# Attention and mixture of experts on one core: all batches projected from raw x, a rebuilt opening, and row normalisation moved to GpSimd

## The chip, the core and the metric

The kernel runs on one core of a Trainium2 chip. The core has five engines with queues of their own: TensorE (PE in the profile, its weight loads PEld), VectorE (DVE), ScalarE (ACT), GpSimd (POOL) and SyncE (SP, which issues most of the DMAs). Each works through its queue in order and waits for the others by semaphores. The metric is the device time of one execution in microseconds (us), the median of several runs.

## What is computed

The input x has 16 batches of 512 tokens of 128 features, float32. Cut to what matters:

```python
xn = layernorm(x)                       # no gain, no bias
q, k, v = xn @ Wq, xn @ Wk, xn @ Wv     # 16 heads of 8
q, k = q / |q|, k / |k|                 # per head
o = causal_softmax(8 * q @ k.T) @ v     # per head
attn = o @ Wo
probs = softmax(xn @ Wr.T)              # 8 experts
top_v, top_i = top_k(probs, 2); top_v = top_v / sum(top_v)
ffn = sum over the two experts e:  top_v[e] * (gelu(xn @ W1[e].T + b1[e]) @ W2[e].T + b2[e])
out = x + attn + ffn
```

## The kernel before, in words

**Layer norm by two roads.** The mean is taken out of the weights: `centre` (L325) subtracts the columns' means from `wall` (Wq, Wk, Wv side by side) and from the router's `wr_sb`. Batches 0 to 3 (`b < RAW`) are normalised row by row first (`normalise`, L302), turned by TensorE (`turn_x`, L315) and projected; their copies out of PSUM are plain. Batches 4 to 15 arrive a second time as 32x32 squares (`load_squares`, L120), are turned in place by VectorE (`turn_raw`, L321), and projected raw; `rstd` is a scale of the copy out (L675). Every batch's normalised rows are still wanted in `rows`, since these are the rows that go to the experts. `stats` (L237) takes the statistics of one batch on VectorE (four instructions), and `scales` (L264) makes `rstd` and `shift` of a range of batches: `variance`, then the root by ScalarE's Sqrt and a reciprocal, or (`root=False`) by a logarithm and an exponential and one Newton step.

**Preparing a batch** (`prep`, L653): `proj` of four pieces of 128 tokens (TensorE, copied out by ScalarE), `squares` of queries and keys (GpSimd), `values` into `vaug` (GpSimd), `sums` of squares, `root`, `root_step` and `scale` (VectorE and ScalarE), then `turn_q` and `turn_k` (transposes on TensorE, copied by VectorE), and `alone`, which makes from the turned keys one copy for each of four groups of heads.

**The loop over stages.** A batch's attention is PER = 10 stages; stage t belongs to batch t // 10. In each, `scores` (L757) runs the `sim` matmuls and two exponentials on ScalarE (L787), `mask` (L803) zeroes the upper triangles of the diagonal blocks of the stage before, on GpSimd or, for some stages, on VectorE, and `weigh` (L821) multiplies two stages later by the values into the one bank `av`, which VectorE then turns into `mid` (L833). A mask goes to VectorE only when the list `router` is empty. The order on every engine is the order in which this program is written: `at_stage(t, step)` puts a step into `plan`, and `due(t)` runs the steps of stage t after its `weigh`. `prep(b)` places its steps from eighteen stages before the batch to one after its start. The list `side` gives one step to each stage from 0 on: turns of x and, for groups of four batches, `logits` (matmuls with the router's weights) and `turn_logits`. Projections, transposes and logits share one PSUM bank, `misc`; scores and some early steps rotate over three double banks (`SIM`).

**The router.** `route` (ten steps) picks two experts for each token, `place` (eight steps, then `later`) counts them and gives each row its slot. A list of (stage, steps) spreads these over stages 20 to 38, nearly all of it VectorE's. From stage 40 on, `stage` takes one or two of 128 `sends` (indirect DMAs by GpSimd that write `rows` to the slots in DRAM). GpSimd's work runs in the order of issue (`on_pool`, L592). Before stage 138 the last sends are flushed, and SP starts to fetch the experts' blocks (L898 to L919), which wait for all sends. The experts run before stage 140 (`hidden`, L950, and `mix`, L964), and the last two batches' attention and the combination end the kernel.

**The opening.** Ahead of stage 0 stands an order written out by hand for batch 0 (`zero`): statistics, normalisation by ScalarE and VectorE, transposes, projection, norms, turned queries and keys, and in between statistics of batches 1 to 7 and normalisation of batches 1 to 4. `keep_busy` runs matmuls whose results nobody reads. `InstLoadActFuncSet` (L1168) loads the function table for the exponentials.

Of the kernel before, what the change touches and what calls it, by code (L numbers as in the profile page):

```python
# [24 lines left out]
def attention_moe_kernel(  # L25
# [276 lines left out]
    def normalise(b, engines):  # L302

        for c, engine in enumerate(engines):
            i = b * NC + c
            to, what = rows[b][:, c, :D], x_sb[b][:, c]
            by, less = rstd[:, i : i + 1], shift[:, i : i + 1]
            if engine is nc.scalar:
                nc.scalar.activation(to, what, AF.Identity, bias=less, scale=by)
            elif engine is nc.vector:  # L310
                nc.vector.tensor_scalar(to, what, by, less, ALU.mult, ALU.add)
            else:
                on_pool(nc.gpsimd.tensor_scalar, to, what, by, less, ALU.mult, ALU.add)

    def turn_x(b, bank, copy):  # L315

        for c in range(NC):
            nc.tensor.transpose(bank[:, ts(c, P)], rows[b][:, c, :D], ident)
        copy(xnT[b], bank)  # L319
# [5 lines left out]
    def centre():  # L325

        means = SIM("means")
        for w, first in ((wall, 0), (wr_sb, NQKV)):
# [3 lines left out]
        return lambda: [  # L332
            nc.vector.scalar_tensor_tensor(
# [8 lines left out]
    def logits(b0):  # L342
# [7 lines left out]
        nc.vector.tensor_copy(ltT, lt)  # L350

    def turn_logits(b0):
# [6 lines left out]
        if b0 < RAW:  # L359
            nc.vector.tensor_copy(to, what)  # L360
        else:
            by = rstd[:, b0 * NC : (b0 + GB) * NC].rearrange("p (g c) -> p c g", g=GB)
            nc.vector.tensor_mul(
                to, what, by.unsqueeze(3).to_broadcast([P, NC, GB, E])
            )
# [292 lines left out]
    def prep(b):  # L658
# [5 lines left out]
        def proj(c, bank=misc):  # L664
# [6 lines left out]
            if b < RAW:  # L671
                nc.scalar.copy(s["qkv"][:, c], pp[:, :NQKV])  # L672
            else:
                i = b * NC + c
                nc.scalar.activation(  # L675
                    s["qkv"][:, c], pp[:, :NQKV], AF.Identity, scale=rstd[:, i : i + 1]
                )
# [18 lines left out]
        def sums():  # L696
            s["ss"] = sm.tile([P, n], F32, tag="ss", name=f"ss{b}", bufs=1)
            nc.vector.tensor_reduce(
                s["ss"].rearrange("p (c h) -> p c h", c=NC), heads(s["qkn"]), AX.X, ALU.add
            )  # L700
            nc.vector.tensor_scalar_max(s["ss"], s["ss"], L2_EPS * L2_EPS)

        def root_now(meanwhile):
# [3 lines left out]
            meanwhile()  # L707
# [11 lines left out]
        def scale():  # L719
            nc.vector.tensor_mul(  # L720
                heads(s["qkn"]),
                heads(s["qkv"][:, :, : 2 * D]),
                s["rn"].rearrange("p (c h) -> p c h", c=NC).unsqueeze(3).to_broadcast(
                    [P, NC, 2 * HEADS, DH]
                ),
            )

        def turn_q():
# [4 lines left out]
            nc.vector.tensor_copy(s["qT"], pt)  # L733

        def turn_k(bank=misc):
# [4 lines left out]
            nc.vector.tensor_copy(s["kr"], pt)  # L740
# [12 lines left out]
        times = (-18, -17, -14, -11) if b > 1 else (-11, -11, -10, -9)  # L753
# [331 lines left out]

    count_up = scratch("count_up", NT + NB + 2 * E).bitcast(I32)
    first = 0
    for to, base, step, per_partition in (
        (rows_all[:, :, D], 0, 2 * P, 2), (iota_b[:, :ND], 1, 2, 0),
        (iota_b[:, ND:], 2 * ND, 1, 0), (iota_e, 0, 1, 0), (back_e, E, -1, 0),  # L1090
    ):
        n = to.shape[1]
        count = count_up[:, first : first + n]
        nc.gpsimd.iota(
            count, pattern=[[step, n]], base=base, channel_multiplier=per_partition
        )
        nc.vector.tensor_copy(to, count)
        first += n

# [6 lines left out]

    keep_busy(3)
    centred = centre()
    stats(0)
    for step in scales(0, 1, True):  # L1110
        step()
# [18 lines left out]
    for t in vaugs:  # L1130
        nc.gpsimd.memset(t, 0.0)
        nc.gpsimd.memset(t[:, :, :, DH : DH + 1], 1.0)


    ACT, POOL, DVE = nc.scalar, nc.gpsimd, nc.vector
    zero = prep(0)
    normalise(0, (ACT, ACT, DVE, DVE))
    centred()
    turn_x(0, SIM("xnt0"), nc.scalar.copy)
    for b in range(1, 4):  # L1140
        stats(b)
    variance, shifts = scales(1, 4, True)
    for c in range(NC):
        zero.proj(c, SIM if c else misc)
        zero.squares(c)
        if c == 1:
            variance()
            stats(4)
            shifts()
    keep_busy(2, wall)  # L1150
    normalise(1, (ACT,) * NC)
    stats(5)
    stats(6)
    zero.values(0)
    zero.values(2)
    normalise(3, (POOL,) * NC)
    zero.sums()
    zero.root_now(lambda: stats(7))
    turn_x(1, SIM("xnt1"), nc.scalar.copy)
    keep_busy(2, wall)  # L1160
    normalise(2, (ACT,) * NC)
    turn_x(2, SIM("xnt2"), nc.scalar.copy)
    zero.scale()
    keep_busy(1, wall)
    variance, shifts = scales(4, 8, True)
    variance()
# [3 lines left out]
    )  # L1170
    zero.turn_q()
    zero.turn_k(SIM)
    zero.alone(0)
    zero.alone(1)
    shifts()
    normalise(4, (POOL,) * NC)
    for t in range(3):
        at_stage(t, lambda t=t: normalise(5 + t, (ACT, POOL, POOL, POOL)))
    at_stage(0, lambda: zero.alone(2))
    at_stage(1, lambda: zero.alone(3))  # L1180
# [3 lines left out]
    def turn(b):  # L1184
        if b < RAW:
# [38 lines left out]
    def stage(t, b, n):  # L1224
# [11 lines left out]
        if side:  # L1236
            side.pop(0)()
# [91 lines left out]
```

## Time and profile before

| what | value |
|---|---|
| median of 3 runs | 722.94 us (722.15 to 723.16) |
| the profiled execution | 720.24 us |
| its span in the profile | 718.5 us |
| first scores (stage 0) | 24.71 us |
| start of stage 10 / 20 / 30 / 40 | 55.45 / 85.61 / 112.63 / 143.30 us |
| granted clock of TensorE | 0.995 |

The profile is of one execution; its span lies 1.7 us under that execution's device time, and that 2.7 us under the median of the other runs. A timeline's row gives start, duration, engine, line, operation, `out<-in` by the program's names and how many instructions are merged in it, and in brackets the engine's idle time before it with what ended that. A row of the busy times by stretch gives the stretch, its length, and the busy microseconds (with the number of instructions) of PE, PEld, DVE, ACT and POOL, then the granted clock, the DMA engines' share and GB/s. A group of instructions ends with busy microseconds, mean nanoseconds of one, and idle time before. A line of waits ends with the total in us, the times, and the longest. All of GpSimd's operations in the loop have line L609, a helper's. Names without a number stand for all batches.

### The profile page before, as it was taken

How to read it: one execution, taken by the hardware profiler on the slowest of the kernel's cores; microseconds unless marked ns; L12 is line 12 of the kernel's file. 1: busy time of each engine (PE TensorE's matmuls, PEld its weight loads, DVE VectorE, ACT ScalarE, POOL GpSimd, SP SyncE). 2: the span in 40 equal slices, each digit the busy share in tenths (PEclk: the TensorE clock that was granted, in tenths of full speed). 3: DMA queues.
4: the chain of work that ended last, by engine and by line, in shares of the span. 5: the costliest groups of instructions: out<-in, count | busy, mean ns of one | idle time of the engine just before them, and what ended most of it. 6: DMA issues, size and time to landing. Idle time of an engine off the chain costs nothing.

```text
span 718.5 us, 16873 instructions
## 1 busy us (share of the span) xinstructions
PE 693.7 (97%) x6224; PEld 423.8 (59%) x6224; DVE 486.9 (68%) x1068; ACT 472.5 (66%) x732; POOL 459.8 (64%) x545
## 2 busy tenths in 40 slices
PE   7899999999999999999999998999999999999996
PEld 3344443444444444444443478999989999998442
DVE  8866579898898887677677734645455554544497
ACT  3778687687787788888888843444444444445873
POOL 5669445488888889887877234555546556545553
PEclk9999999999999999999999999999999999999998
DMA  9888810011111110111110699999999999894794
GB/s 223 212 235 247 238 49 1 2 32 35 37 33 35 35 40 31 39 39 32 39 36 31 133 123 247 249 242 253 250 240 262 236 238 244 237 255 120 248 346 118
DMA packets 171283, 103.21 MB, mean 144 GB/s; under 512 B 124077, under 2 KB 155952, under 8 KB 171202
## 3 DMA queue, kind: packets, MB, share of 16 engines
q1 hardware_dynamic: 161922, 84.80, 47.9%
q0 software_dynamic: 8416, 17.06, 7.0%
q8 instruction: 49, 0.80, 0.5%
q10 hardware_dynamic: 864, 0.28, 0.2%
q14 instruction: 32, 0.26, 0.1%
HBM read 71.73 MB, written 35.54 MB: 149 GB/s over the span
## 4 chain that ended last, share of the span: by engine, by line
PE 72%; SPq 7%; DVE 7%; POOL 6%; issue 3%; DMA 3%; ACT 1%; DVEq 0%; POOLq 0%; ACTq 0%
PE sim L777 17%; PE av L821 16%; PE av L964 16%; PE ph L950 15%; PE proj L668 5%; POOL slots L609 4%; SPq L907 3%; SPq L122 3%; DVE x L1058 2%; PE po L865 1%; POOL ex L609 1%; PE qt L731 1%; SPq L102 1%; DVE mid L833 1%; PE kt L738 1%
## 5 line engine op out<-in xcount | busy, mean ns | idle before, releaser
L787 ACT ACTIVATE ex<-sim 128x1024 f32<-128x1024 f32 x320 | 310.1, 1022 | 79.7 <-PE sim L777 75.2
L609 POOL DMA_INDIRECT results<-y,to x135 | 132.4, 981 | 122.8 <-DVE y L972 90.1
L955 ACT ACTIVATE xnT<-ph,bias 128x256 f32<-128x256 f32 x284 | 108.5, 465 | 139.0 <-PE ph L950 119.2
L777 PE MATMUL sim<-qT,kT 32*128 32x512 f32 (+3 forms) x2048 | 190.2, 460 | 0.5 <-ACT ex L787 0.5
L821 PE MATMUL av<-ex,vaug 128*12 128x512 f32 (+3 forms) x2048 | 169.4, 435 | 5.3 <-DVE mid L833 3.1
L609 POOL DMA_INDIRECT slots<-rows,pos x128 | 145.3, 1135 | 30.7 <-issue 29.1
L609 POOL TENSOR_SCALAR_AFFINE_SELECT ex<-ex 128x512 f32<-128x512 f32 (+1 forms) x119 | 103.7, 879 | 79.8 <-ACT ex L787 76.7
L777 PEld LDWEIGHTS sim<-qT,kT 32*128 32x128 f32 x2048 | 96.1, 183 | 77.5 <-issue 37.1
L964 PEld LDWEIGHTS av<-w,xnT 128*128 128x128 f32 x1080 | 132.4, 193 | 5.3 <-ACT xnT L955 1.9
L950 PE MATMUL ph<-xgT,w 128*128 128x256 f32 (+1 forms) x568 | 129.4, 371 | 5.4 <-DMA w<-packed 3.3
L964 PE MATMUL av<-w,xnT 128*128 128x128 f32 x1080 | 133.5, 277 | 0.9 <-DVE mid L833 0.9
L821 PEld LDWEIGHTS av<-ex,vaug 128*12 128x12 f32 x2048 | 43.4, 91 | 118.2 <-issue 66.0
L950 PEld LDWEIGHTS ph<-xgT,w 128*128 128x128 f32 x568 | 99.4, 191 | 16.7 <-DVE kT L746 3.4
L969 DVE TENSOR_TENSOR y<-av,w 128x256 f32<-128x256 f32 x71 | 29.2, 411 | 113.0 <-PE av L964 113.0
L833 DVE STREAM_TRANSPOSE mid<-av 128x512 f32<-128x512 f32 x64 | 45.6, 712 | 51.6 <-PE av L821 51.4
L799 DVE TENSOR_TENSOR ex<-ex,causal 128x1024 f32<-128x1024 f32 (+1 forms) x63 | 70.0, 1110 | 4.5 <-ACT ex L787 4.3
L668 PE MATMUL proj<-wall,xnT 128*128 128x384 f32 x128 | 57.6, 536 | 2.7 <-DVE xnT L319 0.8
L609 POOL TENSOR_TENSOR qkn<-qkv 128x256 f32<-128x256 f32 x64 | 42.9, 682 | 8.3 <-ACT qkv L672 6.7
L746 DVE TENSOR_SCALAR kT<-kr,hmask 128x512 f32<-128x512 f32 x64 | 39.7, 623 | 0.6
L668 PEld LDWEIGHTS proj<-wall,xnT 128*128 128x128 f32 x128 | 19.3, 188 | 29.0 <-issue 18.6
L928 DVE STREAM_TRANSPOSE xgT<-z 128x256 f32<-128x256 f32 x71 | 30.1, 424 | 5.6 <-DMA z<-slots 5.2
L972 DVE TENSOR_TENSOR y<-y,gate 128x256 f32<-128x256 f32 x71 | 29.3, 413 | 2.4
(170 smaller groups left out, 498.9 us busy)
## 6 DMA issues: line engine op xcount, KB each, us to landing
w<-packed SPq DMA_DIRECT2D x71, 576.0 KB
slots<-fill SPq DMA_DIRECT2D x45, 198.0 KB
z<-slots SPq DMA_DIRECT2D x256, 32.0 KB
xnT<-results SPq DMA_DIRECT2D x10, 512.0 KB
x<-in_x_dram SPq DMA_DIRECT2D x16, 256.0 KB
out_dram<-x SPq DMA_DIRECT2D x15, 256.0 KB
xnT<-in_x_dram SPq DMA_DIRECT2D x48, 64.0 KB
yt<-results SPq DMA_DIRECT2D x6, 512.0 KB
```

The lines of the kernel that those rows point to most:

```text
L609: ins = op(*args, **kw)
L668: nc.tensor.matmul(pp[:, :NQKV], xnT[b][:, ts(c, P)], wall, start=True, stop=True)
L746: nc.vector.tensor_scalar_mul(s["kT"][:, r], s["kr"], hmask[:, r : r + 1])
L777: nc.tensor.matmul(halves[g // 2][:, g % 2, col : col + (NC - j) * P], s["kT"][group, r, ts(j, P)], s["qT"][group, j * P :], start=True, s ...
L787: nc.scalar.activation(ex[:, 2 * h : 2 * h + 2], half, AF.Exp, scale=SCALE)
L799: nc.vector.tensor_mul(diag, diag, causal.unsqueeze(1).unsqueeze(1).to_broadcast([P, NG, many, P]),)
L821: nc.tensor.matmul(av[32 * g : 32 * g + VW, j * P :], s["vaug"][:, j, NG * g + r], s[m][:, g, col : col + (NC - j) * P], start=(j == 0), s ...
L833: nc.vector.transpose(s["mid"][:, r], av)
L928: nc.vector.transpose(s["xgT"], s["z"])
L950: nc.tensor.matmul(ph[:, m], s["w1"][:, ts(m, P)], s["xgT"], start=True, stop=True)
L955: nc.scalar.activation(s["gT"][:, m], ph[:, m], AF.Gelu, bias=bias1[:, i, m : m + 1])
L964: nc.tensor.matmul(py[:, c], s["gT"][:, m, ts(c, P)], s["w2"][:, m], start=(m == 0), stop=(m == NM - 1),)
```

## The change

All sixteen batches are projected from raw x. Batches 0 to 3 are turned by TensorE from `x_sb` instead of from `rows`, all four in the opening, and their copies out are scaled by `rstd`, as are the logits of all groups. Normalisation is no part of any chain to the scores: all 64 pieces are made by GpSimd, two of them in each of two successive stages for a batch, from stage 3 (batch 0) to stage 38 (batch 15).

The opening is written anew: x0's transposes come before its statistics; the centring is cut in two; only batches 0 and 1 have their scales made there; the sum of squares is cut in two; batch 1's first two projections stand ahead of batch 0's scaling in the program; the scaling is cut in keys and queries, keys first. The turned queries and keys of batches 0, 1 and 2, and the logits of all groups, are copied out of PSUM by ScalarE rather than VectorE. Four of the eight groups of filler matmuls go. `vaug` is cleared by VectorE, the second buffer in stage 0; the constants counted out by GpSimd (`count`) move to stage 9.

In the stages, one batch's statistics come at a time, with three calls of `scales` by logarithm (batch 2; 3 to 7; 8 to 15) in stages 1 to 22. `side` becomes a table by stage: turns of batches 4 to 15 from stage 3 to 22, logits in 9, 13, 18 and 23. Batch 2's first two projections come one stage later. The router takes stages 26 to 40, and `sends` may go as soon as there are any.

The diff's core:

```diff
-    def normalise(b, engines):
-        for c, engine in enumerate(engines):
+    def normalise(b, half):
+        for c in (2 * half, 2 * half + 1):
...
-            if engine is nc.scalar:
-                nc.scalar.activation(to, what, AF.Identity, bias=less, scale=by)
-            elif engine is nc.vector:
-                nc.vector.tensor_scalar(to, what, by, less, ALU.mult, ALU.add)
-            else:
-                on_pool(nc.gpsimd.tensor_scalar, to, what, by, less, ALU.mult, ALU.add)
+            on_pool(nc.gpsimd.tensor_scalar, to, what, by, less, ALU.mult, ALU.add)
...
-            nc.tensor.transpose(bank[:, ts(c, P)], rows[b][:, c, :D], ident)
+            nc.tensor.transpose(bank[:, ts(c, P)], x_sb[b][:, c], ident)
...
-        nc.vector.tensor_copy(ltT, lt)
+        nc.scalar.copy(ltT, lt)
...
-            if b < RAW:
-                nc.scalar.copy(s["qkv"][:, c], pp[:, :NQKV])
-            else:
-                i = b * NC + c
-                nc.scalar.activation(
-                    s["qkv"][:, c], pp[:, :NQKV], AF.Identity, scale=rstd[:, i : i + 1]
-                )
+            i = b * NC + c
+            nc.scalar.activation(
+                s["qkv"][:, c], pp[:, :NQKV], AF.Identity, scale=rstd[:, i : i + 1]
+            )
...
+        turned_copy = nc.scalar.copy if b < 3 else nc.vector.tensor_copy
...
-        times = (-18, -17, -14, -11) if b > 1 else (-11, -11, -10, -9)
+        times = (-11, -11, -10, -9) if b == 1 else (-18 + (b == 2), -17 + (b == 2), -14, -11)
...
+    clear(0)
     zero = prep(0)
-    normalise(0, (ACT, ACT, DVE, DVE))
-    centred()
+    keep_busy(2)
     turn_x(0, SIM("xnt0"), nc.scalar.copy)
-    for b in range(1, 4):
-        stats(b)
-    variance, shifts = scales(1, 4, True)
+    centre_all, centre_router = centre()
+    stats(0)
+    variance, shifts = scales(0, 1, True)
+    variance()
+    centre_all()
+    turn_x(1, SIM("xnt1"), nc.scalar.copy)
+    shifts()
+    centre_router()
+    stats(1)
+    variance, shifts = scales(1, 2, True)
     for c in range(NC):
         zero.proj(c, SIM if c else misc)
         zero.squares(c)
         if c == 1:
             variance()
-            stats(4)
+            zero.sums(0, 2)
             shifts()
...
+    turn_x(2, SIM("xnt2"), nc.scalar.copy)
+    turn_x(3, SIM("xnt3"), nc.scalar.copy)
     zero.values(0)
     zero.values(2)
...
+    zero.sums(2)
+    zero.root_now()
     nc.scalar.add_instruction(
         mybir.InstLoadActFuncSet(name=nc.get_next_instruction_name(), act_func_set_id=6)
     )
+    keep_busy(2, wall)
+    prep(1)
+    ahead = plan.pop(-1)
+    for step in ahead[:2]:
+        step()
+    zero.scale(HEADS)
+    zero.turn_k(SIM)
+    zero.scale(0, HEADS)
     zero.turn_q()
-    zero.turn_k(SIM)
     zero.alone(0)
     zero.alone(1)
...
+    side = {
+        t: (lambda step=step, b=b: step(b))
+        for step, at in (
+            (turn_raw, {
+                3: 4, 4: 5, 6: 6, 7: 7, 12: 8, 14: 9, 16: 10, 17: 11, 19: 12, 20: 13, 21: 14,
+                22: 15,
+            }),
+            (logits, {13: 0, 9: 4, 18: 8, 23: 12}),
+            (turn_logits, {15: 0, 11: 4, 25: 8, 24: 12}),
+        )
+        for t, b in at.items()
+    }
+    some = [scales(b0, b1, False) for b0, b1 in ((2, 3), (3, 8), (8, B))]
...
+    for b in range(B):
+        t = (3, 5, 7, 11, 13, 15, 17, 19)[b] if b < 8 else 23 + 2 * (b - 8)
+        for half in range(2):
+            at_stage(t + half, lambda b=b, half=half: normalise(b, half))
...
-        (20, (0,)), (22, (1,)), (23, (2,)), (24, (3,)), (27, (4,)), (28, (5, 10)),
-        (29, (6,)), (30, (11,)), (31, (7, 12)), (32, (8,)), (33, (13,)), (34, (14,)),
-        (35, (15,)), (36, (16,)), (37, (17,)), (38, (9,)),
+        (26, (0,)), (27, (1,)), (28, (2,)), (29, (3,)), (30, (4,)), (31, (5, 10)),
+        (32, (6,)), (33, (11,)), (34, (7, 12)), (35, (8,)), (36, (13,)), (37, (14,)),
+        (38, (15,)), (39, (9, 16)), (40, (17,)),
...
-                if sends and t >= 4 * PER:
+                if sends:
```

## The prediction

> **What bounds the kernel now.** I read the page first, then the timeline of the first 26 us on every engine, then busy time by stretch, where a stretch is ten stages of the attention loop (a stage begins at its first `sim` matmul), then instruction groups of single stretches, then PE's waits.
>
> ```profile
> PE 693.7 (97%) x6224; PEld 423.8 (59%) x6224; DVE 486.9 (68%) x1068; ACT 472.5 (66%) x732; POOL 459.8 (64%) x545
> ...
> PEclk9999999999999999999999999999999999999998
> ```
>
> PE is busy 97% of the span at full clock: time comes off only where PE idles or does filler. Busy time by stretch (stages 0-9, 20-29, 30-39, 40-49 and 80-89):
>
> ```profile
> 24.70:55.40 30.70, 29.48 (x273) 12.95 (x272) 23.34 (x68) 23.93 (x36) 23.59 (x44) 1.00 0.89 235
> 85.60:112.60 27.00, 27.00 (x285) 11.83 (x284) 20.07 (x33) 21.16 (x26) 13.81 (x19) 1.00 0.24 70
> 112.60:143.30 30.70, 29.77 (x287) 12.39 (x287) 27.26 (x58) 22.14 (x29) 15.16 (x21) 1.00 0.01 2
> 143.30:171.70 28.40, 26.81 (x281) 11.59 (x280) 24.58 (x36) 22.33 (x28) 24.05 (x24) 1.00 0.10 32
> 252.40:278.80 26.40, 26.40 (x284) 11.39 (x284) 21.51 (x31) 21.92 (x27) 22.98 (x24) 1.00 0.12 37
> ```
>
> The numbers after the stretch's length are PE, PEld, DVE, ACT, POOL. A steady ten stages take 26.4 us with PE never idle, so nothing is to be had there. In the first forty stages PE idles under 3 us, all its excess over 4 x 26.4 being real matmuls. What is left is the opening, in which PE waits or runs fillers until the first scores at 24.71:
>
> ```profile
> 17.51 0.31 ACT L706 ACTIVATE ss<-ss 128x128 f32<-128x128 f32 x1 [1.28 <-DVE ss L701]
> ...
> 21.65 1.28 ACT L1168 ACT_TABLE_LOAD   x1
> ...
> 23.86 0.91 PE L668 MATMUL proj<-wall,xnT 128*128 128x384 f32 x2 [0.57 <-ACT qkv L672]
> 24.71 1.14 PE L777 MATMUL sim<-qT,kT 32*128 32x512 f32 x8
> ```
>
> **The opening, step by step.** Before: statistics of x0 at 4.14, four normalisations at 7.27, transposes at 7.82, projection at 9.43, copies out until 13.6, norms' sum at 16.02 (DVE was in other batches' statistics, 14.47 to 16.10), root 17.51, scaling 19.14 to 20.37, turned copies to 22.9, first scores 24.71.
> After, x0 itself is turned, so only the weights and the scale of the copies out wait for statistics. The first `vaug`'s clearing, now DVE's (POOL took 0.9), ends before x0 is there at 4.14, after DVE's last step at 2.35. PE: two fillers, x0's transposes about 5.3 to 6.2, the means matmuls as before at 6.4 to 7.46. DVE centres `wall` (0.55) by 7.9. x1's transposes (0.66) end at 8.1, and the first projection starts there: 1.3 us earlier than 9.43. From there I keep the durations of before: one copy out after 0.95; two squares on POOL 1.25; on DVE four statistics 0.86, then the variance of batch 1, 1.75 (it took 10.80 to 12.64 beside the squares, its two-input steps going from 0.17 to 0.6). Its root stands in ACT's queue ahead of the third copy out, at 11.4; the copies end at 12.7 (0.55 each, scaled), squares at 13.4, the second half of the sum 0.6 and the maximum 0.23 at 14.3. So the root comes at 14.3, against 17.51.
> Then: root 0.31, reciprocal 0.93, keys' half of the scaling 0.65, to 16.25. But ACT loads its table (1.28) at 14.6, and only then copies out batch 1's first piece (15.95 to 16.5); batch 1's second piece shares that PSUM bank and sits in PE's queue ahead of the keys: 16.55 to 17.45. Keys' transposes to 18.1, queries' to 18.75, their copies on ACT to 18.75 and 19.4. First scores at about 19.45: **5.3 us earlier**. Bounds: 7 us if the keys are not held behind that piece; 3.2 us if ACT needs a second table load (1.28, the same row) because a copy is now its first instruction, and DVE meets POOL more often. I take 5.3, as each term has a row.
>
> **Stages 0 to 9.** PE's work there falls: one pair of logits instead of two (8 matmuls, 1.41 in the timeline, each), no turn of logits instead of two (0.6 each), batch 3's transposes gone (0.66): 29.3 becomes 26.05. What took PE's place in the cover is ACT: 20 exponentials 19.4 (as in this stretch before), six copies out at 0.58, 3.5, two turned copies and one of logits at 0.6 (its copy of x0's transposes took 0.59), 1.8, and roots by logarithm 1.5: 26.2 us of ACT, its normalisations gone, against 26.05 of PE. Three half-stages of PSUM lie between them, so I charge 1 us of stalls where PE meets a bank that ACT has not yet emptied. Before lost 1.4 here.
>
> **Stages 10 to 40.** The moved logits come back: 3 pairs at 1.41 and 4 turns at 0.6 beside 3.3 for the router's two matmul steps, 89.05 us of PE work (before 86.4, and 87.85 measured). Two queues fill:
> POOL. Its normalisations are 64 instead of 41; in stages 23 to 38 there are now two a stage, where before there were none.
>
> ```profile
> L609 POOL TENSOR_SCALAR rows<-x,rstd,shift 128x128 f32<-128x128 f32 x37 | 17.1, 476 | 7.6 <-DVE shift L296 7.4
> ```
>
> That is 0.95 a stage: 13.81 + 6.7 of 27 us and 15.16 + 8.5 of 30.7, about 77%, under the 87% of stages 80-89, where PE loses nothing. Behind them in POOL's queue stand the causal masks, whose readers are PE's `av` matmuls two stages on. I charge nothing for the load itself.
> DVE. The router takes 15 stages (26 to 40) instead of 19. Ten steady stages hold 21.51, less 6.7 of masks (on POOL until the router is through) and 2.7 of expert biases: 12.1. The router is then 20.07 + 27.26 - 24.2 - 1.3 = 21.8. So 18.2 + 21.8 = 40.0 us of DVE stands against 42.8 of PE. Queued behind router steps are the transposes `mid`, for which the single bank `av` and so PE's next `av` matmuls wait. Stage by stage it fits, but from the transposes of stage 39 to those of 41 (gates, moved, choose) it is about 1 us over.
> What POOL's extra reads do to DVE is the open term:
>
> ```profile
> L387 DVE TENSOR_TENSOR val<-val,back_e x2: 719/1096/1472, 93.8 to 108.2; 128x512 f32<-128x512 f32 x2
> ```
>
> The same product took 719 and 1472 ns. The Trainium skill ("SBUF — State Buffer", "Who interferes with whom") speaks against the change here: a VectorE instruction with two SBUF inputs and a GpSimd one that reads SBUF exclude each other for a whole instruction. By the rule about 16 such products meet a normalisation in 0.35 of the cases for up to 0.45: 2.5 us more of DVE; at the row's fast end, nothing. I take 1.3, so 41.3 of 42.8, and 2.5 us of stalls in all for stages 10 to 40 (1.4 before), between 1.4 and 5.
> The statistics, one batch a stage (0.86), and the cleared second `vaug` (about 0.9) fall in stages 0 to 20 on a DVE that was 62% busy in stages 10-19; they are covered, and cost their own length where a `mid` waits behind them. The counts' five casts in stage 9 wait for POOL's iotas and hold DVE perhaps 1.5 us, inside that stage's 3.9 us.
>
> **Fillers.** Four of the eight filler groups go. The skill ("TensorE: Matmul & The Clock Gate", "What's actually happening") says the clock halves after an idle window of about 3.4 us. The widest PE gap in the opening is 1.24 us with the clock at 1.00, and mine are 0.9 and 0.7; by the row nothing, by the rule, if a gap grows past it, one such window at half speed, 1.7 us. I take nothing.
>
> **Sends.** The slots are chosen in stage 40 rather than 37, and sends start in stage 41. One send fewer by every later stage moves the last from 134 to 135, but POOL has no work with a wait between those two places, so the first fetch behind it stays. POOL's first send may wait for the slots with a mask behind it: 0.4. SP's loads keep their order; batch 8's turn comes at stage 12 (about 51 us), its four loads are issued by 26.2.
>
> **Sum.** Opening +5.3; stages 0 to 40: before 118.6 (24.71 to 143.30), after 26.05 + 1 + 89.05 + 2.5 = 118.6, so 0; sends -0.4: **4.9 us less**. The profiled execution took 720.24 (span 718.5 and 1.7 around it), 2.7 under the median of 722.94; 4.9 off either gives 715.3 for such an execution and **718.0** for the median.
>
> **Rivals.**
> Larger gain: the keys do not wait behind batch 1's piece and ACT keeps up: opening 7, one us of stalls less: 722.94 - 7 - 1 + 0.4 = 715.3. For it: DVE is done with the keys at 16.25. Against: PE's queue is in order.
> Nothing: the second table load and the meetings on the port leave the opening 3.2; stages 0 to 9 stall 2 us and 10 to 40 3.6, together 2.1 more than in the sum; with the send's 0.4 only 0.7 is left: 722.2. For it: ACT and PE are equal to 0.2 us in stages 0 to 9.
> Slower: late masks, in stages 23 to 40, where normalisations stand ahead of them in POOL's queue.
>
> ```profile
> PE av L821 <- POOL ex L609: 1.9, 5, 0.7
> ```
>
> That is PE's wait in stages 40 to 69, with sends of 1.1 us in that place: five times, 0.38 each, 0.7 at most. If all 18 stages paid p, the kernel is slower by 18p - 6.0 (4.9, and 1.1 for the stalls that the sum already adds there): even at p = 0.33, slower by 0.2% above 0.41; at 0.5 it gives 725.9. For it: the same kind of wait. Against: five in thirty stages, at a higher POOL load, and a normalisation is half as long as a send.
>
> **How the numbers follow.** Forecast 0.64 (718.0, alone 716.0 to 720.6), larger gain 0.12, nothing 0.10, slower 0.14. A measurement of this kernel can tell about 0.2%, 1.45 us. So faster 0.76, same 0.10, slower 0.14. The range runs from the larger gain's value to just past no change, 715.0 to 723.4, which leaves out most of the slower case and the tail of the larger gain.
>
> **What would show it.** First `sim` near 19.5; the root of batch 0 near 14.3; `proj` of batch 1 between it and the keys' transposes; stage 40 near 138; ACT the engine with the least slack in stages 0 to 9; DVE over 95% in stages 26 to 40; `av` waiting for `mid` more than for POOL; stretches from stage 70 on, the experts and the tail unchanged. It is wrong if first scores come after 22, if PE waits for POOL's masks in most stages from 23 to 40, or if the experts' first weights arrive later against stage 140 than before.

## The result: 780 us, and where the profile puts it

The changed kernel takes **780.27 us** (median, 780.08 to 780.68) where the kernel before takes 722.55 beside it: a ratio of 1.081 (95% interval 1.078 to 1.084). The forecast was 718.0. The profiled execution took 780.42, span 778.6.

The page's row of PE and its slices, as they were read for the kernel before:

```profile
PE 690.4 (89%) x6216; PEld 423.6 (54%) x6216; DVE 484.1 (62%) x1074; ACT 473.0 (61%) x726; POOL 472.3 (61%) x566
...
PE   0008999998899999999999999799999999999996
...
PEclk9999999999999999999999999899999999999999
```

PE does 3.3 us less work than before (693.7) and was 97% busy, now 89%: the first three slices of 19.5 us are empty. PE's waits name what ended them (total, times, longest):

```profile
PE idle L1083 <- DMA xnT<-in_x_dram: 56.8, 1, 56.8
PE av L816 <- POOL ex L599: 5.7, 8, 2.3
PE ph L945 <- DVE kT L741: 4.7, 1, 4.7
```

One wait of 56.8 us, and it belongs to a *filler*. In the kernel before, the same wait ended after 1.5 us:

```profile
PE idle L1103 <- DVE wr_sb L109: 1.5, 1, 1.5
```

(The third line names `kT` for 4.7 us. It stands at the same matmul at which the kernel before, e1 and e14 below wait for fetched weights, `PE ph <- DMA w<-packed`, and is read as that wait.) The timeline around the end of the 56.8 us (start, us, engine, line, operation, tiles, and in brackets the idle time before):

```profile
52.63 2.07 SPq L122 DMA_DIRECT2D xnT<-in_x_dram  x4
54.75 2.48 SPq L1094 DMA_DIRECT2D slots<-fill  x5
...
56.79 4.18 PE L1083 MATMUL idle<-xnT 128*128 128x512 f32 x4 [56.79 <-DMA xnT<-in_x_dram]
```

`keep_busy` multiplies `spare` by itself, and `spare` is no tile of its own: line 94 makes it `xnT2[-1][:, 0]`, the half tile in which batch 14's squares land. The kernel before wrote `keep_busy(3)` ahead of the loop that fills the slots and, in it, loads the squares of the late batches (L1091 of the changed kernel). The change wrote `keep_busy(2)` behind that loop. In program order the filler now reads what batch 14's load writes, so it must wait for it; those loads stand far back in SP's queue and are issued at 52.63. The transposes of x0 stand behind the fillers in PE's queue. VectorE begins on x0 at 4.10 us, so x0 was there, but PE turns it at 60.76: it waits behind matmuls whose results nobody reads.

The same five stretches as before (PE, PEld, DVE, ACT, POOL after the length):

```profile
74.90:102.90 28.00, 26.88 (x256) 11.93 (x256) 21.16 (x60) 23.75 (x32) 20.51 (x40) 1.00 0.33 103
133.60:163.80 30.20, 28.67 (x300) 12.57 (x299) 22.90 (x52) 22.74 (x30) 21.01 (x34) 1.00 0.01 1
163.80:197.60 33.80, 30.43 (x291) 12.68 (x290) 29.87 (x58) 22.74 (x29) 26.98 (x41) 1.00 0.01 1
197.60:228.60 31.00, 26.68 (x282) 11.38 (x281) 25.35 (x40) 22.13 (x27) 23.49 (x24) 1.00 0.09 28
309.30:335.70 26.40, 26.40 (x285) 11.39 (x284) 21.51 (x30) 21.91 (x27) 22.99 (x25) 1.00 0.12 37
```

The steady stretch is the same to 0.1 us. Stages 30 to 50 hold 7.7 us of idle PE (33.80 + 31.00 less 30.43 and 26.68), where the kernel before had 2.5: a second, smaller loss, which the total alone would not show. And the opening itself, once the fillers are through, is the one forecast:

```profile
69.74 0.31 ACT L698 ACTIVATE ss<-ss 128x128 f32<-128x128 f32 x1 [0.84 <-DVE ss L693]
70.07 1.28 ACT L1154 ACT_TABLE_LOAD   x1
...
72.00 0.91 PE L658 MATMUL proj<-wall,xnT 128*128 128x384 f32 x2 [1.23 <-ACT qkv L662]
...
74.91 1.14 PE L772 MATMUL sim<-qT,kT 32*128 32x512 f32 x8 [0.68 <-DVE kT L741]
```

From the fillers' end (60.97) it is 8.8 us to the root and 13.9 to the first scores; the forecast had 14.3 and 19.45 with fillers to 5.3, that is 9.0 and 14.15.

One thing to know for what follows: on the chips of e5 to e8, of e9 to e11 and of e13 the kernel before itself took 750 to 753 us (in these runs' traces ScalarE and VectorE stand still together for some us at places where no releaser shows, and PE's clock falls to half behind it; the traces of e6, e7 and e13 are moreover of slow executions), so these runs are given as ratios to it, and read by single stages.

### The profile page after: what moved, and what is told of

It is laid out like the page before. It is cut to its first block, busy times and chain, and to the rows that moved or that the text cites. A ratio compares the mean times of both kernels' runs of the same rounds, so it can differ in the third digit from the quotient of the medians.

```text
span 778.6 us, 16867 instructions
## 1 busy us (share of the span) xinstructions
PE 690.4 (89%) x6216; PEld 423.6 (54%) x6216; DVE 484.1 (62%) x1074; ACT 473.0 (61%) x726; POOL 472.3 (61%) x566
## 4 chain that ended last, share of the span: by engine, by line
PE 64%; SPq 9%; POOL 8%; DVE 8%; issue 4%; ACT 3%; DMA 2%; DVEq 0%; ACTq 0%; POOLq 0%
PE sim L772 15%; PE av L959 14%; PE ph L945 13%; PE av L816 13%; PE proj L658 4%; POOL slots L599 4%; SPq L122 3%; SPq L902 3%; POOL ex L599 2%; ACT ex L782 2%; DVE x L1053 2%; SPq L1094 2%; PE po L860 2%; DMA z<-slots 1%; POOL qkn L599 1%
## 5 line engine op out<-in xcount | busy, mean ns | idle before, releaser
L945 PEld LDWEIGHTS ph<-xgT,w 128*128 128x128 f32 x568 | 100.3, 193 | 18.5 <-DVE kT L741 4.9
L1083 PE MATMUL idle<-xnT 128*128 128x512 f32 x4 | 4.1, 1134 | 56.8 <-DMA xnT<-in_x_dram 56.8
L662 ACT ACTIVATE qkv<-proj,rstd 128x384 f32<-128x384 f32 x64 | 37.1, 581 | 7.8 <-PE proj L658 7.3
L314 ACT COPY xnT<-xnt 128x512 f32<-128x512 f32 x4 | 2.2, 585 | 56.1 <-PE xnt L313 56.1
```

What stands on the lines that cost most here:

```text
L662: nc.scalar.activation(s["qkv"][:, c], pp[:, :NQKV], AF.Identity, scale=rstd[:, i : i + 1])
L945: nc.tensor.matmul(ph[:, m], s["w1"][:, ts(m, P)], s["xgT"], start=True, stop=True)
```

## The experiments

Theory A: the filler's tile is the cause, by the order of the program. Rival B: the new order of loads or of the opening is slow in itself, and the fillers are only what PE happens to stand at. In the diffs `...` marks lines left out, and a comment behind `#` that names a run was added here.

**e1, the fillers ahead of the loads** (also the base of e5 to e14)

```diff
+    keep_busy(2)
     fill = scratch("fill", NR * ROW).rearrange("p (r w) -> p r w", w=ROW)
...
-    keep_busy(2)
     turn_x(0, SIM("xnt0"), nc.scalar.copy)
```

> The changed kernel with one line moved: the first two fillers stand ahead of the loads of batches 8 to 15 in the program, as they did before the change; TensorE's own order is the same. Theory A (the fillers read the tile that batch 14's squares are loaded into, so behind that load in the program they wait for it, and all of TensorE's queue with them): TensorE starts near 1.5 us instead of 56.8, first scores near 19.2 (74.91 less 55.7), and the time falls by about 55.7, to 724.6, if the stalls that the changed kernel shows after its first scores (stages 9 to 44, the experts' first block: about 10 us more than before) are its own; to 718 if they came from the late start. Rival B (the opening is late because of the loads of x, or of another wait that the late fillers only happen to stand at): TensorE's first work moves to 1.5 us but the transposes of x0 still start near 60, and the time stays near 780.

729.62 us (before beside it 721.14; ratio 1.0118, 1.0095 to 1.0141). First scores 20.02. The 56.8 us wait is gone; rival B falls. But 718 is not reached.

**e2, the kernel before with its fillers behind the loads**

```diff
-    keep_busy(3)
-    centred = centre()
     stats(0)
...
+    keep_busy(3)
+    centred = centre()
     ACT, POOL, DVE = nc.scalar, nc.gpsimd, nc.vector
```

> The kernel before with this alone: its three first fillers and the means stand behind the loads of batches 8 to 15 in the program. Theory A: TensorE's first instruction waits for batch 14's squares, near 56.8 us as in the changed kernel, first scores near 79 (24.7 plus about 55), about 777 in all. Rival B: as before, 722.

774.97 us (one run). The old kernel falls into the same hole by two lines:

```profile
PE idle L1103 <- DMA xnT<-in_x_dram: 57.8, 1, 57.8
```

**e3 and e4, the order of the change, another tile**

```diff
-    spare = xnT2[-1][:, 0]
+    spare = xnT2[4][:, 0]     # e3: batch 8, whose squares are loaded halfway
+    spare = xnT2[0][:, 1]     # e4: batch 1, which is loaded with no squares
```

> The changed kernel with its order untouched; only the tile that the first fillers read is another: the half that batch 8's squares are loaded into, whose four loads SyncE issues by 25.2 us instead of 54.7. Theory A: the wait follows the tile; TensorE starts near 27, 30 us earlier, and the time is near 751. Rival B: 780, since order and loads are the same.

> The changed kernel with its order untouched; the first fillers read batch 1's half, which no load ever writes. Theory A: no wait at all, the same time as with the fillers moved (724.6, or 718 if the later stalls came from the late start). Rival B: 780.

e3 750.66 (one run), e4 729.46 (ratio 1.0111, 1.0086 to 1.0136). e3's wait:

```profile
PE idle L1083 <- DMA xnT<-in_x_dram: 28.5, 1, 28.5
```

The start of PE follows the load of whichever batch owns the tile: 56.8, 28.5, and with no load 1.5. Theory A is shown, and e1 and e4 agree to 0.2 us though one mends the order and the other the tile. The filler costs 50.7 us (780.27 less 729.62), not the 55.3 that PE starts late: in e1 stages 10 to 19 take 4.4 us more than in the changed kernel (35.17 against 30.77), for a wait that the late start had covered and that is looked at next.

What is left is the 1.2% by which e1 is slower than the kernel before. By stretches, in the profiled executions of before and of e1 (span 718.5 and 728.0):

| stretch | before | e1 | difference |
|---|---|---|---|
| opening | 24.71 | 20.02 | -4.7 |
| stages 0-9 | 30.74 | 27.95 | -2.8 |
| stages 10-19 | 30.16 | 35.17 | +5.0 |
| stages 20-29 | 27.02 | 30.18 | +3.2 |
| stages 30-39 | 30.67 | 33.77 | +3.1 |
| stages 40-49 | 28.43 | 31.03 | +2.6 |
| stages 50-138 | 236.5 | 237.0 | +0.5 |
| stage 139, to the first scores of 140 | 251.6 | 254.3 | +2.7 |
| the rest | 58.7 | 58.6 | -0.1 |

In stages 10 to 19 POOL shows the reason (e1's timeline):

```profile
44.08 0.63 POOL L599 TENSOR_SCALAR_AFFINE_SELECT ex<-ex 128x512 f32<-128x512 f32 x1 [0.79 <-ACT ex L782]
52.33 0.59 POOL L599 IOTA count_up<- 128x64 int32 x5 [7.62 <-PE lg L351]
52.86 1.20 POOL L599 TENSOR_TENSOR qkn<-qkv 128x256 f32<-128x256 f32 x2
54.02 1.43 POOL L599 TENSOR_SCALAR_AFFINE_SELECT ex<-ex 128x512 f32<-128x512 f32 x2
```

`count`, a step that needs no data at all, idles POOL for 7.62 us: its `count_up` takes a buffer of `scratch`, which has two, and one is held by `fill` (SP still reads it at 67 us), the other by the turned logits of batches 4 to 7, read last in stage 11. Masks stand behind it. In the changed kernel, where the loop began 55 us later, SP was done with `fill` by then, and `count` (at 99.7 us) waited for nothing.

**e5, `count` from stage 9 to stage 16**

```diff
-        9: [some[1][1], count],
+        9: [some[1][1]],
+        16: [count],
```

> The run with the two fillers ahead of the loads (729.6 us), and in it the step `count` (five index tables by GpSimd, cast by VectorE) moved from stage 9 to stage 16. Theory: `count` takes a buffer of `scratch` that is still held by `fill` or by the transposed logits of batches 4 to 7, so GpSimd idles 7.6 us there and the masks behind it hold PE's values in stage 11 (6.2 us) and 12 (3.8 us). Then stage 11 falls back to about 2.7 and stage 12 to about 2.9 us, stages 10 to 20 take about 30.8 in place of 35.2, and the whole about 725.1 us. Rival: the masks are late from GpSimd's own load of rows to send: stages 11 and 12 stay, and the time stays at 729.5.

Stage 11 fell from 6.18 to 2.65 us, 12 from 3.77 to 2.90, stages 10 to 19 from 35.17 to 30.76: as the theory had it. (Ratio 1.0095, 1.0064 to 1.0127.)

**e6, a send more in ten stages; e7, the sends two stages later; e8, rows by ScalarE** (each on e5)

```diff
-            for _ in range(2 if t % PER in (4, 5, 7) or t % (2 * PER) == 2 else 1):
-                if sends:
+            for _ in range(2 if t % PER in (4, 5, 7, 8) or t % (2 * PER) == 2 else 1):   # e6, e7
+                if sends and t > 4 * PER + 2:                                           # e7
...
-            on_pool(nc.gpsimd.tensor_scalar, to, what, by, less, ALU.mult, ALU.add)
+            if b < 8:                                                                   # e8
+                on_pool(nc.gpsimd.tensor_scalar, to, what, by, less, ALU.mult, ALU.add)
+            else:
+                nc.scalar.activation(to, what, AF.Identity, bias=less, scale=by)
```

> As the run with `count` in stage 16, and one send more in every ten stages (a second one in stages 8, 18, ...), so that the last send stands some six stages earlier than 134. Theory: the last scores' wait for the first weights fetched (4.9 us, `PE ph <- DMA w<-packed`) comes from the last sends standing too close to the end: it falls to 1 to 3 us, and the time by 2 to 4 us to about 722 to 723. Rival: the fetch is held by the backlog of the queue that it stands in, not by the last send: wait and time unchanged, about 725.

> As the run before it (a send more in ten stages), and the first send two stages later, behind stage 42, where before the change the sends began at 40 with their positions at hand. Theory: GpSimd's first send waits for the positions (`pos`) in stage 42 and the masks of stages 42 to 44 stand behind it: these stages fall from 5.5 and 3.9 us to about 3.1 and 3.0, and the time by about 3.3 us, to 719 to 720. Rival: the stages are long because VectorE's positions themselves hold its queue: no change of those stages, about 722.5.

> As the run with `count` in stage 16, and the rows to send of batches 8 to 15 (stages 23 to 38, 32 operations of 0.67 us) made by ScalarE in place of GpSimd. Theory: GpSimd's load in these stages puts the masks off, and with it stages 32, 33 and 38 (3.6, 5.3, 6.7 us): stages 30 to 40 fall by 1 to 2.5 us from 33.8. Rival: VectorE's router steps are what comes late there (`kt` waits for `qT`, scores for `kr`): stages 30 to 40 as they were, or longer by what ScalarE now comes late with, up to 1 us.

e6: ratio 0.989 (0.978 to 1.000). The wait for the fetched weights, 4.8 us in e5, is gone, as the theory had it (for `xgT` PE waits 2.6 us, in e1 2.0). e7: 0.994 (0.989 to 1.000). Stage 44 fell from 3.87 to 2.72 us, but 42 did not fall (5.52 to 6.55, with the clock at half in part of it): with POOL free, PE waits there 1.8 us for `mid`, which stands behind VectorE's slots, and stage 45 grew from 2.48 to 3.94: stages 40 to 49 took 33.6 us in all, where e6 had 31.2. Its rival was right on the sum. e8: 1.014 (1.007 to 1.021); stages 30 to 39 take 35.2 us where e5 had 34.0, not less: GpSimd's normalisations are not what stalls PE there, as the rival had it.

**e9, the router over stages 26 to 44, and e12, sends only from stage 47** (on e6)

```diff
-        (26, (0,)), (27, (1,)), (28, (2,)), (29, (3,)), (30, (4,)), (31, (5, 10)),
-        (32, (6,)), (33, (11,)), (34, (7, 12)), (35, (8,)), (36, (13,)), (37, (14,)),
-        (38, (15,)), (39, (9, 16)), (40, (17,)),
+        (26, (0,)), (27, (1,)), (28, (2,)), (29, (3,)), (30, (4,)), (32, (5,)),
+        (33, (10,)), (34, (6, 11)), (35, (7, 12)), (36, (13,)), (38, (14,)),
+        (40, (15,)), (41, (8,)), (42, (9,)), (43, (16,)), (44, (17,)),
...
-            for _ in range(2 if t % PER in (4, 5, 7, 8) or t % (2 * PER) == 2 else 1):
-                if sends:
+            for _ in range(2 if t % PER in (2, 4, 5, 7, 8) else 1):
+                if sends and not router:                # e9
+                if sends and t > 4 * PER + 6:           # e12
...
-        if later and t > 4 * PER + 2 and t % PER in (0, 5, 7):
+        if later and t > 4 * PER + 8 and t % PER in (0, 5, 7):
```

> As the run with `count` in stage 16 and a send more in ten stages, and the router's sixteen steps spread over stages 26 to 44 in place of 26 to 40, none beside another heavy step of VectorE; the sends begin behind the last of them, two of them in five stages of ten. Theory: VectorE is busy for all of stages 32, 33, 36 to 38 and 42 with router steps put closer than before the change, and PE idles there 6.7 us in stages 30 to 50 (0.4, 1.0, 1.8, 2.3 and 1.1 of it in stages 32, 33, 38, 42 and 44) against 1.6 before: the idle time of these stages falls to 2 to 3 us and the time by 3 to 4 us, to 718.5 to 720 where the kernel before takes 721 (a ratio of 0.996 to 0.999). Rival: the stalls are set by something else (masks on GpSimd behind rows to send, clock): idle time of 30 to 50 stays over 5 us, ratio 1.002 or more.

> As the run with the router's steps spread over stages 26 to 44, but the sends begin in stage 47, when VectorE has made the positions, not in 45, where GpSimd's first send waited for them with the masks behind it (`PE av <- POOL ex`, 2.9 us in stage 46, and PE's clock at half behind it). Theory: stage 46 falls from 7.3 to about 2.9 us, PE's idle time in stages 30 to 50 to under 3 us, and the time stands 0.3 to 0.7% below the kernel before: about 717 to 719 where that takes 721. Rival: the wait moves on to the end, whose last sends now stand as late as before the change (`PE ph <- DMA w<-packed` 3 us or more), and the ratio is 1.000 or more.

e9: 1.022 (1.015 to 1.029): stage 40 began at 139.8 (143.3 in e6), then a send waited for its slots with the masks behind it, and stage 46 took 7.3 us. e12: **727.80 us** (before 722.48; 1.0081, 1.0058 to 1.0104). Its stretches of stages 30-39 and 40-49:

```profile
108.90:139.70 30.80, 28.02 (x287) 11.71 (x286) 26.81 (x52) 22.59 (x29) 25.93 (x41) 1.00 0.01 1
139.70:168.30 28.60, 28.57 (x287) 12.00 (x286) 21.25 (x38) 21.84 (x27) 16.86 (x22) 1.00 0.04 14
```

Against e1 that is 5.4 us less. PE's idle time in the two stretches falls from 7.7 to 2.8 us, but mostly in the second (4.3 to 0.03), where masks had stood behind the waiting send; in stages 30 to 39 it falls only from 3.4 to 2.8, and these are shorter because PE's router matmuls have moved behind stage 40. So the spread of the router itself is worth little. At stage 40 this kernel is 3.7 us *ahead* of the one before, and from stage 139 to 140 it gains 4.9 more. Yet it is slower, and one wait says why:

```profile
PE av L816 <- POOL ex L599: 17.1, 18, 1.5
PE av L816 <- DVE mid L828: 2.2, 4, 0.8
```

From stage 57 to 129 most stages ending in 7 took 3.23 us (before: 2.64), and those ending in 9 took 4.03 (before: 2.47). With 15 sends in ten stages POOL has no slack, and the mask that `av` needs stands behind two of them (timeline of stage 59):

```profile
192.61 0.95 POOL L599 DMA_INDIRECT slots<-rows,pos  x1 [0.30 <-issue]
193.87 0.96 POOL L599 DMA_INDIRECT slots<-rows,pos  x1 [0.30 <-issue]
194.84 1.11 POOL L599 TENSOR_SCALAR_AFFINE_SELECT ex<-ex 128x1024 f32<-128x1024 f32 x1
196.00 0.62 PE L816 MATMUL av<-ex,vaug 128*12 128x256 f32 x8 [1.49 <-POOL ex L599]
```

POOL's busy share does not show this: it is 87% in stages 80 to 89 both here and before. The idle rest is what counts. POOL's waits in these ten stages, before and in e12:

```profile
POOL slots L609 <- issue: 3.3, 14, 0.3
POOL slots L599 <- issue: 3.6, 15, 0.3
```

Work and these 0.24 us ahead of each send make 26.3 of 26.4 us before (22.98 + 3.3) and 28.5 of 28.6 in e12 (24.90 + 3.6). POOL waits for no other engine in either: it was full already in the kernel before, and with a fifteenth send the ten stages take 2.2 us more.

**e10, a root as ScalarE's first operation; e11, logits copied by VectorE as before the change** (on e6)

```diff
+    first = const.tile([P, 1], F32, name="first_root")    # e10, behind ScalarE's loads
+    nc.vector.memset(first, 1.0)
+    nc.scalar.activation(first, first, AF.Sqrt)
...
-        nc.scalar.copy(ltT, lt)
+        nc.vector.tensor_copy(ltT, lt)                 # e11
```

> As the run with `count` in stage 16 and a send more in ten stages, and one square root of a [128, 1] tile as ScalarE's first operation, so that the copy of the first transposed batch finds a table that has both and the second table load (1.28 us at 7.2 us) falls away. Theory one: the second load holds the first square root and with it the scale of the first projection: the first scores come 0.3 to 1.3 us earlier than 20.0. Theory two: the centring of the weights (VectorE at 8.1 us, behind PE's sums of them) comes later than the root in any case: the first scores stay within 0.2 us of 20.0. The whole, on a chip where the kernel before takes 721: 722 to 723 (ratio 1.000 to 1.003), which also gives the time of the two edits below it.

> As the run with `count` in stage 16 and a send more in ten stages, and the four copies of router logits out of PSUM (`ltT`) made by VectorE as before the change, not by ScalarE. Theory: PE's projections wait for a bank that ScalarE frees late in stages 9, 13 and 23 (4.55 us each, `proj <- ACT ltT`, 2.3 us in all); then these stages fall to about 3.8 and the whole by 1.5 to 2.3 us. Rival: VectorE is as late there: the stages stay within 0.3 us, and the time stays at 722 to 723.

e10: ratio 0.988 (0.979 to 0.997); first scores at 19.45 with the second table load gone (root at 6.40, `rstd` at 8.21). e11: 0.989 (0.981 to 0.997); first scores at 19.45 *with* that load (root at 7.82). So it costs nothing, and 19.45 against 20.09 in e6 has another reason: in e6, as in e1, x0's four transposes take 1.06 us in place of 0.60, at half clock. e11's stages 9, 13, 18, 22 and 23 take 22.2 us together, e6's 22.0 (stage 9 grew by 0.9, stage 13 fell by 0.45): in the sum the rival had it, VectorE is as late there. e6, e10 and e11 have no run on a chip on which the kernel before takes 722; why they are faster than it where it takes 750 stays open.

**e13, two of four squarings by ScalarE; e14, 14.5 sends in ten stages** (each on e12)

```diff
-            on_pool(nc.gpsimd.tensor_mul, s["qkn"][:, c], qk, qk)
+            if c > 1 and b > 4:                                                           # e13
+                nc.scalar.activation(s["qkn"][:, c], qk, AF.Square)
+            else:
+                on_pool(nc.gpsimd.tensor_mul, s["qkn"][:, c], qk, qk)
...
-            for _ in range(2 if t % PER in (2, 4, 5, 7, 8) else 1):
+            for _ in range(2 if t % PER in (0, 1, 4, 5, 7) else 1):                       # e13
+            for _ in range(2 if t % PER in (4, 5, 7, 8) or t % (2 * PER) == 2 else 1):    # e14
```

> As the run whose sends begin in stage 47 (727.8 us), and GpSimd relieved: from batch 5 on two of a batch's four squarings of its queries and keys are made by ScalarE, and the two further sends of every ten stages stand in stages 0 and 1 of ten, where those squarings stood, not in 2 and 8. Theory: what keeps that run above the kernel before is GpSimd, full with 15 sends in ten stages: its masks are late in stages 57, 59, 67, 69 and so on to 129 (`PE av <- POOL ex`, 17.1 us in all, some 0.6 and 1.5 us in a seventh and ninth stage), while the opening, stages 30 to 50 and the end are each ahead of before. Then that wait falls under 6 us and the time to 713 to 717, a ratio of 0.987 to 0.994. Rival: ScalarE, busy with two exponentials in most stages, comes late with the squarings or the projections' copies instead: waits of PE for ScalarE of 8 us or more in place of GpSimd's, and a ratio of 1.000 or more.

> As the run whose sends begin in stage 47 (727.8 us), but with 14.5 sends in ten stages in place of 15 (the second send in stage 2 of ten only in every other ten), so that the last stands near stage 135 instead of 132. Theory: GpSimd at 15 sends has no slack, so that each ten stages lose 2.1 us (0.6 in the seventh, 1.5 in the ninth); at 14.5 only every other ten does: about 8 us of the 17.1 us of `PE av <- POOL ex` go, and 1 to 3 come back at the last scores, whose fetch starts later: 720 to 722 where the kernel before takes 722, a ratio of 0.996 to 1.001. Rival: the loss follows the length of GpSimd's queue since the first send, not its rate: 15 us or more of that wait stay, ratio over 1.005.

e13: 1.0066 (1.0036 to 1.0096). The wait for GpSimd fell to 4.4 us, and PE waits 10.8 us for `mid` and 10.6 for ScalarE's exponentials. The rival had named ScalarE, but on such chips e5 to e9, without this edit, show 6.6 to 14.3 and 4.8 to 6.3 us of the same waits; so how much of them is the squarings' stays open, and the ratio alone says that the edit did not bring the forecast gain. e14: **727.41 us** (before 722.31; 1.0077, 1.0063 to 1.0091). Half came true, and the other half was larger than expected:

```profile
PE av L816 <- POOL ex L599: 9.1, 11, 1.5
PE ph L945 <- DMA w<-packed: 5.4, 1, 5.4
```

Stage 139 begins 9.1 us earlier than in e12 and takes 8.1 us longer: PE waits 5.4 for fetched weights, and behind that its clock is at half for 6.8 us. Rate and end are one account. The wait is not for the first weights. In the kernel before, in e1 and in e14 it ends at the same matmul, the first of the sixth `hidden`, where PE arrives 22.1 us into stage 139:

| | before | e1 | e14 | e12 |
|---|---|---|---|---|
| from the start of POOL's last send to stage 139 | 13.0 | 11.3 | 10.6 | 18.5 |
| PE arrives at the sixth `hidden` behind that send | 35.1 | 33.4 | 32.6 | 40.6 |
| PE waits there | 3.3 | 4.9 | 5.4 | none |
| sum | 38.4 | 38.3 | 38.1 | |

So these weights come some 38 us behind the last send, and PE waits for what its own work doesn't cover. In e12 its work covers them; the 0.6 us that it still waits for weights stand six `hidden` later.

## Why the prediction was wrong, point by point

**"PE: two fillers, x0's transposes about 5.3 to 6.2": the step that failed.** I moved an instruction and priced its length, not what it reads; a wait for its operand stood in the sum at nothing. The fillers were weighed only for what they do to the clock, and the row that mattered was their operand: L94, in the code that I had. PE started at 56.79 us and turned x0 at 60.76. 50.7 of the 57.7 us are this (e1, e4; e2 and e3 from the other side). My slower rival, late masks in stages 23 to 40, was the wrong mechanism: the changed kernel loses 0.41 us to them there, in stage 32. The other steps, below, account for the 8.5 us by which e1 is still slower than the kernel before.

**The opening, 5.3 us earlier: right, step by step.** With the accident removed 4.7 (e1), and 5.0 to 5.6 where the first transposes run at full clock (e4, e8, e10, e11, e14). In e11 the root comes at 14.28 (forecast 14.3), the table load at 14.61 (14.6), batch 1's first copy at 15.90 (15.95) and the first scores at 19.45 (19.45). The second table load, which my "nothing" rival priced, is there and costs nothing.

**Stages 0 to 9, 26.05 + 1: nearly right.** 27.94 in the changed kernel: 26.83 of work and 1.11 of idle time.

**Stages 10 to 40, 89.05 + 2.5: the work right, the stalls too small.** In the changed kernel PE works 88.9 of these 94.7 us and idles 5.8. Its larger waits stand in single stages: 13 and 23 (0.7 each, a bank that ScalarE empties late), 22 (0.8, `mid`), 33 (1.0) and 38 (1.8, where PE and VectorE wait for each other in turn over turned queries, keys and slots). In e1 `count` ("inside that stage's 3.9 us") adds 4.4, by a wait for a buffer and not for data, so that the stretch takes 99.1. I had summed VectorE's load over stages 26 to 40, 41.3 of 42.8, and charged 2.5 for what doesn't fit; a mean over a stretch says nothing about an engine that is late in three of its stages. Nor does a full stage alone: VectorE is 96 to 99% busy in stages 30 to 33 and 37, but it was 99% busy in 29, 30, 37 and 38 of the kernel before too, and PE lost only 0.8 us there. The causes of these stalls are read from the waits; no run took them away. The spread of the router (e12) left 2.8 of 3.4 us of idle time in stages 30 to 39.

The meetings of VectorE and GpSimd for SBUF, which I priced at +1.3 us by the Trainium skill's "SBUF — State Buffer" ("Who interferes with whom"), did not grow. The router's fifteen large products (512 elements a row) took 14.1 us in the kernel before and 11.6 in the changed one. Those of 0.94 us and more stand beside a mask or a squaring of GpSimd's, in both kernels (one of them beside a normalisation as well). Three products that lie wholly beside normalisations took 650, 677 and 677 ns, no longer than those with GpSimd idle (680 to 693); a fourth, of another operation, took 766. The page's rule speaks of any GpSimd instruction that reads SBUF; for the normalisations, which do, this trace does not show it.

**GpSimd's normalisations, "nothing for the load itself": right** in stages 23 to 38 (0.41 us of late masks; e8).

**Sends, "the first fetch behind it stays", -0.4: wrong by 5 us** (stages 40 to 49 and 139 in the table). In e1 the first send waits for its slots until 153.4, stage 42 (before: 144.6, stage 40), and stages 42 and 44 lose 3.4 us to the masks behind it; the wait for the weights grows from 3.3 to 4.9, with the clock at half for 6.8 us behind it in place of 3.4. I had held that POOL has no wait between the two last places; it has none, but it has one send more, and a send is 1.14 us of its time. Nor was the idle rest of POOL's 87% in stages 80 to 89 room to catch up: it belongs to the sends. What is late next could have been asked: with statistics one batch a stage, the logits end in stage 25, the router in 40, and the sends must be caught up by an engine with no slack. e12 and e14 show both ways of paying.

**In all:** freed of the two accidents, with router and sends laid out anew, the change stands 0.8% above the kernel before (e12, e14). The opening's 5 us are real, and the later sends give them back with interest: in e12 stages 50 to 138 take 252.9 us against 236.5. No run on a chip where the kernel before takes 722 is below it. On chips where that takes 750, e6, e10 and e11 stood 1.1 to 1.2% below it (e6's interval ends at 1.000); their order was not run on the other chips, so whether it gains there is not shown.

## What to carry to other kernels

Before an instruction is moved, list the tiles that it reads and the buffers that it takes, dummies and constants first, and ask who wrote or holds them at its new place: both of this change's accidents are steps that need no data, waiting for a tile that they borrowed. A gain ahead of a chain counts only if the chain's far end comes earlier as well; here a later router made later sends, and the engine that sends had no room to catch up. Judge an engine's room stage by stage, and count the idle time that belongs to its own instructions: GpSimd at 87% busy was full.

## What the runs showed of the hardware

How the clock answers to PE's gaps, in the traces of the kernel before, the changed one, e1 to e4, e12 and e14 (chips where the kernel before takes 722; the last microseconds of the span aside):

| PE's idle gap | clock behind it |
|---|---|
| 1.0 to 1.75 us, standing alone (eight of 1.5 in e12), but for the next row | full |
| 1.44, in the opening of e2 | half for 3.4 us |
| 2.1 (e2) | half for 3.4 us |
| 2.3, stage 42 of the changed kernel and of e1 | full |
| 2.3, the same stage of e3 | half for 3.4 us |
| 2.7, stage 11 of e1 | half for 3.4 us |
| 2.7, the same stage of e4 | full |
| 3.29 (before), 4.38 (e3) | half for 3.4 us |
| 4.74 (changed), 4.95 (e1), 5.05 (e4), 5.42 (e14) | half for 6.8 us |

Two gaps of 1.06 and 0.78 us close together in stage 38 were followed by 6.8 us at half in e4, and by none in e1. So the time at half comes in pieces of 3.4 us, and for gaps of 1.4 to 2.7 us it varied, at the same place in like kernels, whether one came. Half speed for 6.8 us is 3.4 us of lost work, so a wait of 5 us ahead of a dense stretch costs up to 3.4 more than itself. The Trainium skill ("TensorE: Matmul & The Clock Gate", "What's actually happening") has the window, 3.4 us, and that it runs free, which fits the pieces and the variation. It also fits the opening's two forms: behind the same two fillers, x0's transposes took 1.06 us in e1 and e12 and 0.60 in e4, e11 and e14, and the first scores came at 20.0 or at 19.2 to 19.5.
